# Two decoder layers with cross-attention: the attention's hand-written order runs to its end, the prologue's projections are reordered, feed-forward weights overlay the staging, four columns early

## The chip, the cores and the metric

One core of a Trainium2 chip runs the whole program in one launch. The metric is the device time of an execution in microseconds (us); the median of several runs is given. A hardware profile of one execution comes with it. Five engines run their own instruction queues in order: PE (TensorE, matrix products and transposes), DVE (VectorE), ACT (ScalarE), POOL (GpSimd) and SP (SyncE, which here issues all DMA transfers).

## The reference

The input `x` is 8 blocks of 128 tokens by 512 features. Four steps are added to it in turn, each on the layer norm of what is there:

```
x = x + L0_xattn(layernorm(x), ctx)      # one head, keys projected from ctx
x = x + L0_ffn(layernorm(x))             # linear layer plus one LoRA rank, chosen per token
x = x + L1_xattn(layernorm(x), ctx, mask)
x = x + L1_ffn(layernorm(x))
```

The change lies in the last two. `L1_xattn` has 32 query heads and 8 key/value groups of head size 128; within a block of 128 tokens

```
q = rmsnorm(x @ Wq.T) ; k = rmsnorm(ctx @ Wk.T) ; v = ctx @ Wv.T
p = softmax(q @ k.T / sqrt(128) + mask)
out = (p @ v) @ Wo.T
```

`L1_ffn` has integer weights: a matrix is `(w - z) * s`, with one `z` and `s` for each group of 128 input rows and each column. With 1792 hidden features,

```
out = (silu(x @ Wgate) * (x @ Wup)) @ Wdown
```

## The kernel before

Everything is float32 to the outside. A product is made from parts: an operand is cut into a rounded high part (`_h`, a copy on ScalarE) and the remainder (`_l`, a subtraction on VectorE), and `mm3` (lines 73 to 76) adds low x high, high x high and high x low in PSUM. So most cuts consist of a ScalarE instruction and a VectorE instruction that waits for it.

**Attention of the second layer.** The eight blocks are two halves (`hf`) of four. A unit `u` (64 of them, `NU`) is one kv group and one block: four query heads, 128 tokens. Four units share a key block (`k_load`, pool `pk`), a half-group of values (`v_load`) and a weight set of q and o (`wsets`). For one unit there are, in this order:

- `q_mm`: 12 matmuls of 128x512 into a bank of `ps_q` (tile `mm`, two banks); `q_ssq` squares on ScalarE; `q_rms` on POOL; `q_turn` scales and transposes on VectorE; `q_write` and `q_read` carry the result through DRAM, so that it comes back as `qT`.
- `s_mm`: scores, eight small matmuls; `s_max` (mask and maximum, VectorE); `s_exp` (four ScalarE instructions); `s_norm` (reciprocal on VectorE, product on POOL, tile `pr`).
- `p_mm`: four transposes on TensorE (tile `tr`); `p_cut`: `pT_h` on ScalarE, `pT_l` on VectorE; `av_mm`: three matmuls, the third of which reads `pT_l`; `av_cut`: `aT_h`, `aT_l`.
- `o_mm`: 12 matmuls; `o_add` adds to `xs`, the running `x`.

`round_(n)` (line 710) takes these steps for different units from the list `ROUND`, so that a round has one of each: `s_mm(n+1)`, `q_rms(n+3)`, `p_cut(n)`, `q_mm(n+4)` with its first k (three matmuls), `s_max(n+1)`, `av_mm(n)`, `av_cut(n)`, `q_turn(n+3)`, the rest of `q_mm(n+4)`, `s_exp(n+1)`, `o_mm(n)`, `s_norm(n+1)`, `q_ssq(n+4)`, `p_mm(n+1)`, `o_add(n)`. Between them run weight loads (`load`), weight cuts (`cut`: `wst` to the q or o set; pools `pst` and `pwq`/`pwo`), and the making of `w - z` for the feed-forward (`int`, `sub`), which goes to DRAM as `wint`.

**The order.** Inside `with tc.manual_schedule()` every engine's queue has the instructions in the order in which Python wrote them. Outside it a scheduler orders them by its own priorities. Before, the hand order covers a prologue (key/value groups 6 and 7, the first four `q_mm`, `s_mm(0)`) and rounds 0 to 50 (`LAST = 51`); rounds 51 to 63 and the two that follow are ordered by the scheduler. In the prologue each of three iterations has `q_mm(u)` first and then the two `kv_part` (a key/value projection of two blocks, 24 matmuls of 128x256) and `kv_out` (values and transposed keys to DRAM); `kv_w` loads and cuts a group's weights. Key/value groups 0 to 5 are made earlier, in scheduler order.

**The end of attention.** A block is finished when its last unit's `o_add` is done: units 52 to 55 finish the first half, 60 to 63 the second (`norms`). `layernorm_x` (bn_stats and aggr on VectorE, two POOL instructions for `rstd`, then `xn` on VectorE) follows at the end of that round; `layernorm_t` (four transposes into a bank of `ps_q`, `xnT_h` on ScalarE, `xnT_l` on VectorE) three rounds later for the first half, one for the second. With the first half normed, feed-forward columns (128 hidden features each, 14 of them) can begin: `early_unit` (line 634) makes one of four input groups of gate or up for one column, two matmuls of 128x512 into a bank of `ps_q` or `ps_s`; even groups are evacuated by ScalarE (L646), odd ones added on VectorE (L654) or, the last, by ScalarE and POOL (L651, L652); POOL adds the two sums, and tanh and two VectorE products make `early[c]`. `FILL` deals 24 such units (`NE = 3` columns) over the last rounds.

**The feed-forward.** `ORDER` lists the columns. An early column has only its second half of tokens to do. `weights` (L807) loads a column's `wint` into `wf_gate`, `wf_up`, `wf_down` (pool `fw`); `unit` (L816, L817) does its matmuls. Pools of SBUF are opened and closed as stacks from the left and the right, so what a new pool lies over must be free before its first write. Before, `fp` (gate and up sums) and `fw` are opened on the left after attention, in that order.

Of the kernel before, what the change touches and what calls it, by code (L numbers as in the profile page):

```python
# [9 lines left out]
F32 = mybir.dt.float32  # L10
# [7 lines left out]
P = 128  # L18
# [21 lines left out]
def tile_layers(ctx: ExitStack, tc: tile.TileContext, t, out: bass.AP):  # L40
    nc = tc.nc

    def pool(stack, name, bufs, space=None, side="left"):
        kw = {"side": side}
        if space is not None:
            kw["space"] = space
        return stack.enter_context(tc.tile_pool(name=name, bufs=bufs, reuse_waits="tile", **kw))
# [42 lines left out]
    def layernorm_t(xn, nh, nl, cols, ps_tr, extra=None, tag="tr"):  # L90
        tp = ps_tr.tile([P, KT, P], F32, name=tag)
        for k in range(KT):
            nc.tensor.transpose(tp[:, k, :], xn[:, k * P : (k + 1) * P], ident)
        nc.scalar.copy(nh[:, :, cols], tp)
        nc.vector.tensor_tensor(nl[:, :, cols], tp, f32(nh[:, :, cols]), ALU.subtract)
        if extra is not None:
            nc.scalar.copy(extra[:, :, cols], tp)
# [12 lines left out]
    xs = [const.tile([P, HB, D], F32, name=f"xs{hf}") for hf in range(2)]  # L110


    NE = 3
    LAG = 3
    skv = ctx.enter_context(ExitStack())
    cpool = pool(skv, "cpool", 1, side="right")
# [243 lines left out]

    kvw, kvo = {}, {}

    def kv_w(g):
        wst = kvp.tile([P, KT, 2 * HD], F32, name="wkv", bufs=1)
        nc.sync.dma_start(wst, t["kvT"][g].rearrange("(k p) n -> p k n", p=P))
        wh, wl = kvw[g] = tuple(kvp.tile([P, KT, 2 * HD], F32R, name=f"wkv_{p}") for p in "hl")
        for k in range(KT):
            split_fast(wh[:, k, :], wl[:, k, :], wst[:, k, :])
# [40 lines left out]
        nc.sync.dma_start(kT_d[g, hf], kb.rearrange("p j b a -> p j (b a)"))  # L409

    def kv_group(g):
        kv_w(g)
        for hf in range(2):
            for b0_ in (0, 2):
                kv_part(g, hf, b0_)
            kv_out(g, hf)
# [13 lines left out]
    l1s = ctx.enter_context(ExitStack())  # L430

    pst = pool(l1s, "pst", 5)
    pk = pool(l1s, "pk", 3)
    wk = pool(l1s, "wk", 2)
    pwq = pool(l1s, "pwq", 7)
    pv = pool(l1s, "pv", 2)
# [10 lines left out]
            wsets.append((g, HB * j))  # L447
        wset.append(len(wsets) - 1)
    NU = NG * NB
    FILL = {60: 3, 61: 4, 62: 7, 63: 4, 64: 12}  # L450
    xn1 = []
    wq, wo, kTt, vht, vlt = ({} for _ in range(5))
    qps, qss, rqs, qbs, q_d, qTs, sps, nms, sms, prs, tps, pTs, avs, aTs, pos = ({} for _ in range(15))
# [31 lines left out]
    def q_mm(u, ks):  # L485
        j, i = divmod(u, HB)
        v, cols = wset[j], slice(i * P, (i + 1) * P)
        nh, nl = xn1[blocks[j][1]]
        if ks[0] == 0:
            qps[u] = ps_q.tile([P, D], F32, name="mm")  # L490
        for k in ks:
            mm3(qps[u], nh[:, k, cols], nl[:, k, cols], *wq[v, k], k == 0, k == KT - 1)

    def q_ssq(u):
        ssq = qss[u] = small.tile([P, NREP], F32, name="qssq")
        for r in range(NREP):
            junk = wk.tile([P, HD], F32, name="junkq", bufs=2)
            nc.scalar.activation(  # L498
                junk, qps[u][:, r * HD : (r + 1) * HD], AF.Square, accum_out=ssq[:, r : r + 1]
            )  # L500

    def q_rms(u):
        rqs[u] = rms_factor(qss.pop(u), NREP, "q")
# [13 lines left out]
    def q_write(u):  # L517
        q_d[u] = dram.tile([P, NQ, NREP * SQ], F32, name=f"q_d{u}")
        nc.sync.dma_start(q_d[u], qbs.pop(u).rearrange("p j r a -> p j (r a)"))
# [37 lines left out]
    def p_mm(u):  # L557
        tp = tps[u] = ps_tr.tile([P, NQ, P], F32, name="tr")
        for r in range(NQ):
            nc.tensor.transpose(tp[:, r, :], prs[u][:, r, :], ident)  # L560
# [71 lines left out]
        nc.sync.dma_start(f32(et[m, c]), wint[m, c])  # L632

    def early_unit(m, g, c):
        if len(fill) < 10 and g % 2:
            ps = ps_s.tile([P, NREP, P], F32, name="s").rearrange("p r c -> p (r c)")
        else:
            ps = ps_q.tile([P, D], F32, name="mm")
        nh, nl = xn2[0]
        w = et[m, c][:, g * P : (g + 1) * P]  # L640
        nc.tensor.matmul(ps, w, nl[:, g, :], start=True, stop=False)
        nc.tensor.matmul(ps, w, nh[:, g, :], start=False, stop=True)
        s = (sg_sb if m == "gate" else su_sb)[:, c, g : g + 1]
        if g % 2 == 0:
            et[m, c, g] = wk.tile([P, NREP, P], F32, name="qT", bufs=8).rearrange("p r c -> p (r c)")
            nc.scalar.activation(et[m, c, g], ps, AF.Copy, scale=s)  # L646
        else:
            d = et[m, c, g - 1]
            if (m, g) in (("gate",3),("up",3)):
                a2 = wk.tile([P, NREP, P], F32, name="qT", bufs=8).rearrange("p r c -> p (r c)")  # L650
                nc.scalar.activation(a2, ps, AF.Copy, scale=s)  # L651
                nc.gpsimd.tensor_tensor(d, d, a2, ALU.add)  # L652
            else:
                nc.vector.scalar_tensor_tensor(d, ps, s, d, ALU.mult, ALU.add)  # L654
        if g == 3:
            nc.gpsimd.tensor_tensor(et[m, c, 0], et[m, c, 0], et[m, c, 2], ALU.add)
            if m == "gate":
                th = early[c] = fth.tile([P, TOK], F32, name="the")
                nc.scalar.activation(th, et[m, c, 0], AF.Tanh, scale=0.5)
                nc.vector.scalar_tensor_tensor(th, th, 1.0, et[m, c, 0], ALU.add, ALU.mult)  # L660
            else:
                th = early[c]
                nc.vector.scalar_tensor_tensor(th, th, 0.5, et[m, c, 0], ALU.mult, ALU.mult)

    tasks = {}

    def at(n, kind, fn, *a):
        tasks.setdefault((n, kind), []).append((fn, a))
# [13 lines left out]
        at(i, "int", int_dma, m, c)  # L682
        at(i + 1, "sub", int_sub, m, c)

    EW0 = min(FILL) - 2
    for c in range(NE):
        for m in ("gate", "up"):
            at(EW0 + c, "load", early_w, m, c)
    fill = [(m, g, c) for c in range(NE) for m in ("gate", "up") for g in range(KT)]

    def filler(n, k):
        m = FILL.get(n, 0)
        for _ in range(m * (k + 1) // 6 - m * k // 6):
            if fill:
                early_unit(*fill.pop(0))

    xn2, xnb = {}, {}
    norms = {}
    for b in range(NB):
# [8 lines left out]
    ]  # L708

    def round_(n):  # L710
        k = 0
        for it in ROUND:
            if isinstance(it, str):
                for fn, a in tasks.get((n, it), []):
                    fn(*a)
            elif 0 <= n + it[0] < NU:
                it[1](n + it[0], *it[2:])
            if not isinstance(it, str) and it[1] in (s_mm, s_max, av_mm, s_exp, o_mm, p_mm):
                filler(n, k)
                k += 1  # L720
        for b in [b for u, b in norms.items() if u == n - (3 if b < HB else 1)]:
            hf, i = divmod(b, HB)
            if i == 0:
                xn2[hf] = tuple(big.tile([P, KT, TOK], F32R, name=f"xnT_{p}") for p in "hl")
            layernorm_t(xnb[b], *xn2[hf], slice(i * P, (i + 1) * P), ps_q, tag="mm")
        b = norms.get(n)
        if b is not None:
            xnb[b] = layernorm_x(xs[b // HB][:, b % HB, :])

    nc.sync.dma_start(sg_sb, t["gsT"].rearrange("(c p) g -> p c g", p=P))  # L730
# [14 lines left out]
    k_load(*blocks[0])  # L745
    v_load(*blocks[0])


    LAST = 51
    with tc.manual_schedule():  # L750
        kv_w(NG - 2)
        for u, (g, hf) in enumerate(((NG - 2, 0), (NG - 2, 1), (NG - 1, 0))):
            q_mm(u, range(KT))
            q_ssq(u)
            kv_part(g, hf, 0)
            q_rms(u)
            if u:
                q_read(u - 1)
            kv_part(g, hf, 2)
            q_turn(u)  # L760
            q_write(u)
            kv_out(g, hf)
            if u == 0:
                kv_w(NG - 1)
            for k in ((0, 1), (2, 3), ())[u]:
                load_dma("o", 0, k)
        s_mm(0)
        s_max(0)
        s_exp(0)
        q_mm(3, range(KT))  # L770
        q_ssq(3)
        kv_part(NG - 1, 1, 0)
        s_norm(0)
        for fn, a in tasks[-1, "load"]:
            fn(*a)
        kv_part(NG - 1, 1, 2)
        kv_out(NG - 1, 1)
        skv.close()

        fth = pool(ctx, "fth", NE, side="right")  # L780
        pwo = pool(l1s, "pwo", 8, side="right")
        pat = pool(l1s, "pat", 2, side="right")
        ps_tr = pool(l1s, "ps_tr1", 2, PSUM)
        ps_o = pool(l1s, "ps_o", 2, PSUM)
        p_mm(0)
        for k in range(KT):
            load_cut("o", 0, k)
        for n in range(LAST):
            round_(n)
    for n in range(LAST, NU + 2):  # L790
        round_(n)
    l1s.close()

    fh = pool(ctx, "fh", LAG, side="right")
    fa = pool(ctx, "fa", 1, side="right")
    fp = pool(ctx, "fp", 2)
    fw = pool(ctx, "fw", 3)  # L800
    ps_f = pool(ctx, "ps_f", 4, PSUM)

    acc = fa.tile([P, KT, 2, TOK], F32, name="acc")
# [92 lines left out]
        nc.gpsimd.tensor_tensor(first_h[1][:, 0, :], early[c], f32(first_h[0][:, 0, :]), ALU.subtract)  # L896


    ORDER = [3,0,4,1,5]+list(range(6,14))+[2]
    for i in range(NI - NE):  # L900
        O_ = [NE + i] + list(range(NE))[i * NE // (NI - NE) : (i + 1) * NE // (NI - NE)]

    DOWN = {i: (i - LAG,) for i in range(LAG, NI + LAG)}

# [88 lines left out]
```

## Time and profile before

| | |
|---|---|
| runs before, us | 904.38 median of 3 (904.29 to 906.5) |
| the profiled execution, us | 909.4, span 907.6 |
| mean granted TensorE clock | 0.983 |
| TensorE busy | 859.1 us, 95% |
| TensorE weight loads | 722.1 us, 80% |
| VectorE busy | 622.7 us, 69% |
| ScalarE busy | 442.2 us, 49% |
| GpSimd busy | 519.5 us, 57% |
| DMA | 141.07 MB, mean 155 GB/s |

The page lists busy time by engine, then the span in 40 equal slices (a digit is the busy share in tenths; PEclk is the clock that the throttle granted to TensorE, in tenths of full speed), the DMA queues, the chain of work that ended last, and the costliest groups of instructions with what ended the idle time before them. In a timeline, a row has its start, its duration, the engine, the source line, what it writes and reads, and in brackets how long the engine had been idle and which engine's result ended that. In the windows view the columns after the window are its length and the busy time (and count) of PE, PEld, DVE, ACT and POOL, then the granted clock, the DMA engines' busy share and GB/s. Matmuls overlap in their pipeline, so a row's duration is longer than the distance to the next row.

Stages of the profiled execution: the first layer and key/value groups 0 to 5 to about 186 us; the hand-ordered prologue to about 231; the rounds to about 721; the first feed-forward matmul of the last stage starts at 739.08.

### The profile page before, as it was taken

The numbers are of one execution on the slowest core, as the hardware profiler recorded it, in microseconds if no ns is written. First come the engines' busy times: TensorE is split into PE (matmuls) and PEld (weight loads), VectorE is DVE, ScalarE is ACT, GpSimd is POOL, SyncE is SP. The second block draws the span as 40 slices with busy tenths as digits, with TensorE's granted clock in tenths as the row PEclk, the third lists the DMA queues.
The fourth block names the chain that finished last, engine by engine and source line by source line (L and its number), as shares of the span: only waits on it lengthen the run. The fifth ranks groups of instructions, "written<-read, shape, count | busy, mean of one in ns | idle before, by whom it ended". The sixth has DMA issues, their size and how long they took to land.

```text
span 907.6 us, 14436 instructions
## 1 busy us (share of the span) xinstructions
PE 859.1 (95%) x4568; PEld 722.1 (80%) x4568; DVE 622.7 (69%) x1047; ACT 442.2 (49%) x1573; POOL 519.5 (57%) x571
## 2 busy tenths in 40 slices
PE   6999999998899999999999999998999969999985
PEld 5889999888788888888888888886878647788854
DVE  6413897664677776677767766665686647988896
ACT  5324443134444444444444444444465449676652
POOL 4541784222375555555555555867643347899994
PEclk9899999999899999999999999999999979999998
DMA  8422441236787788788777876446421033222102
GB/s 295 127 94 95 151 151 60 82 118 204 231 243 227 228 244 237 222 237 245 232 232 230 236 223 214 138 153 186 150 90 60 0 116 92 65 76 70 47 23 94
DMA packets 141181, 141.07 MB, mean 155 GB/s; under 512 B 17968, under 2 KB 92464, under 8 KB 141104
## 3 DMA queue, kind: packets, MB, share of 16 engines
q1 hardware_dynamic: 141104, 140.14, 50.9%
q8 instruction: 37, 0.61, 0.3%
q14 instruction: 40, 0.33, 0.1%
HBM read 97.62 MB, written 42.47 MB: 154 GB/s over the span
## 4 chain that ended last, share of the span: by engine, by line
PE 68%; issue 9%; POOL 7%; DVE 7%; DMA 6%; ACT 1%; SPq 1%; DVEq 0%; POOLq 0%; ACTq 0%
PE f L816 8%; PE f L817 7%; PE mm L74 7%; PE mm L75 6%; PE mm L76 6%; PE o L76 5%; PE s L533 5%; PE o L74 5%; PE o L75 5%; DMA qT<-q_d 3%; PE tr L560 3%; PE o L574 1%; PE o L572 1%; PE o L573 1%; DMA q_d<-qb 1%
## 5 line engine op out<-in xcount | busy, mean ns | idle before, releaser
L555 POOL TENSOR_TENSOR pr<-pr,rs 128x512 f32<-128x512 f32 x64 | 66.6, 1041 | 163.9 <-DVE rs L553 163.1
L74 PE MATMUL mm<-wq_l,xnT_h 128*128 128x512 f32 x256 | 105.5, 412 | 1.0 <-DVE wq_l L66 1.0
L594 DVE TENSOR_TENSOR xs<-o,xs 128x512 f32<-128x512 f32 x64 | 44.2, 690 | 87.2 <-PE o L76 87.1
L74 PE MATMUL o<-wo_l,aT_h 128*128 128x512 f32 x256 | 100.8, 394 | 2.3 <-ACT aT_h L581 1.3
L76 PE MATMUL o<-wo_h,aT_l 128*128 128x512 f32 x256 | 100.5, 392 | 0.9 <-DVE aT_l L582 0.9
L76 PE MATMUL mm<-wq_h,xnT_l 128*128 128x512 f32 x256 | 100.5, 393 | 0.0
L75 PE MATMUL mm<-wq_h,xnT_h 128*128 128x512 f32 x256 | 100.4, 392 | 0.0
L75 PE MATMUL o<-wo_h,aT_h 128*128 128x512 f32 x256 | 99.8, 390 | 0.0
L547 ACT ACTIVATE pr<-s,nm 128x128 f32<-128x128 f32 x256 | 90.9, 375 | 13.1 <-DVE nm L541 10.7
L564 ACT CAST pT_h<-tr 128x512 fp32r<-128x512 f32 x64 | 37.5, 586 | 112.2 <-PE tr L560 112.2
L581 ACT CAST aT_h<-o 128x512 fp32r<-128x512 f32 x64 | 37.6, 587 | 105.4 <-PE o L574 105.4
L498 ACT ACTIVATE junkq<-mm 128x128 f32<-128x128 f32 x256 | 67.6, 279 | 22.9 <-PE mm L76 16.3
L74 PE MATMUL kv<-wkv_l,cT_h 128*128 128x256 f32 x256 | 73.6, 288 | 0.8 <-DVE kn L396 0.6
L76 PE MATMUL kv<-wkv_h,cT_l 128*128 128x256 f32 x256 | 73.3, 286 | 0.0
L75 PE MATMUL kv<-wkv_h,cT_h 128*128 128x256 f32 x256 | 72.8, 284 | 0.0
L533 PE MATMUL s<-kT,qT 128*128 128x128 f32 x512 | 69.2, 278 | 3.7 <-DMA qT<-q_d 3.7
L533 PEld LDWEIGHTS s<-kT,qT 128*128 128x128 f32 x512 | 63.9, 194 | 5.5 <-issue 3.4
L344 POOL TENSOR_TENSOR rrq<-msq,nhalf 128x4 f32<-128x4 f32 x64 | 65.0, 1016 | 5.0
L74 PEld LDWEIGHTS o<-wo_l,aT_h 128*128 128x128 f32 x256 | 48.1, 188 | 13.5 <-ACT aT_h L581 4.1
L565 DVE TENSOR_TENSOR pT_l<-tr,pT_h 128x512 fp32r<-128x512 f32 x64 | 44.1, 689 | 20.4 <-ACT pT_h L564 20.2
L76 PEld LDWEIGHTS o<-wo_h,aT_l 128*128 128x128 f32 x256 | 48.0, 188 | 12.0 <-DVE aT_l L582 2.2
L76 PEld LDWEIGHTS mm<-wq_h,xnT_l 128*128 128x128 f32 x256 | 48.2, 188 | 10.7
(220 smaller groups left out, 2459.7 us busy)
## 6 DMA issues: line engine op xcount, KB each, us to landing
q_d<-qb SPq DMA_DIRECT2D x64, 256.0 KB, 2.5
qT<-q_d SPq DMA_DIRECT2D x256, 64.0 KB, 3.2
wst<-in_qpT SPq DMA_DIRECT2D x36, 256.0 KB, 3.9
wst<-in_opT SPq DMA_DIRECT2D x36, 256.0 KB, 3.4
wkv<-in_kvT SPq DMA_DIRECT2D x8, 512.0 KB, 4.3
v_d<-vh SPq DMA_DIRECT2D x16, 256.0 KB, 2.1
v_d<-vl SPq DMA_DIRECT2D x16, 256.0 KB, 2.3
kT_d<-kT SPq DMA_DIRECT2D x16, 256.0 KB, 2.6
```

Source lines behind the costliest of these rows:

```text
L74: nc.tensor.matmul(o, ah, bl, start=start, stop=False)
L75: nc.tensor.matmul(o, ah, bh, start=False, stop=False)
L76: nc.tensor.matmul(o, al, bh, start=False, stop=stop)
L344: nc.gpsimd.tensor_tensor(r[:, :n], ms[:, :n], nhalf[:, :n], ALU.pow)
L498: nc.scalar.activation(junk, qps[u][:, r * HD : (r + 1) * HD], AF.Square, accum_out=ssq[:, r : r + 1])
L533: nc.tensor.matmul(sp[:, r, :], qTs[u][:, r, :], kTt[blocks[j]][:, :, i, :], start=True, stop=True)
L547: nc.scalar.activation(pr[:, r, :], sps[u][:, r, :], AF.Exp, bias=nms[u][:, r : r + 1], accum_out=sm[:, r : r + 1])
L555: nc.gpsimd.tensor_tensor(pr, pr, rs.unsqueeze(2).to_broadcast([P, NQ, P]), ALU.mult)
L565: nc.vector.tensor_tensor(pl, tps[u], f32(ph), ALU.subtract)
L594: nc.vector.tensor_tensor(x, pos[u], x, ALU.add)
L816: nc.tensor.matmul(ps[:, hf, :], w, rl, start=True, stop=False)
L817: nc.tensor.matmul(ps[:, hf, :], w, rh, start=False, stop=True)
```

## The change

- Prologue: `kv_w` becomes `kv_load` and `kv_cut`; group 6 is loaded and cut, and group 7 loaded, ahead of the hand order. Each iteration has its first `kv_part` at its head; `q_rms`, `q_turn`, `q_write` of a unit come one iteration later; `q_mm(3)` follows the last `kv_part`; the cuts of the first o set and `q_ssq(3)` come ahead of `p_mm(0)`.
- The hand order covers all 64 rounds, the remaining early units and the last norm. Early units come at two places of a round, after `s_mm` and after `av_mm`: 1 and 3 in rounds 60 to 62, 3 and 3 in round 63, 11 after it, the last norm's transposes, and 3 more. The norm's transposes come one round after `layernorm_x` for both halves.
- `NE` is 4: 32 early units. They take `ps_q` every third time and banks of `ps_s` and `ps_tr` otherwise, and `ps_q` alone from round 63 on. All odd groups are added on VectorE; POOL's sum follows one unit later, the tanh and the products four units later (`later`).
- `pk` has two buffers instead of three. `fw`, `fa`, `fh` are opened on the left in this order, `fp` on the right, so that `fw` lies over the staging tiles (`pst`, `pk`).
- `ORDER` becomes [4,0,5,1,6,2,7,...,13,3] from [3,0,4,1,5,...,13,2].

```diff
-    NE = 3
+    NE = 4
...
-    pk = pool(l1s, "pk", 3)
+    pk = pool(l1s, "pk", 2)
...
-    FILL = {60: 3, 61: 4, 62: 7, 63: 4, 64: 12}
...
     def early_unit(m, g, c):
-        if len(fill) < 10 and g % 2:
-            ps = ps_s.tile([P, NREP, P], F32, name="s").rearrange("p r c -> p (r c)")
+
+        i = len(fill)
+        if i >= LATE or i % 3 == 0:
+            ps = ps_q.tile([P, D], F32, name="mm")
         else:
-            ps = ps_q.tile([P, D], F32, name="mm")
+            p, n = ((ps_s, "s"), (ps_tr, "tr"))[i % 3 - 1]
+            ps = p.tile([P, NQ, P], F32, name=n).rearrange("p r c -> p (r c)")
...
-            if (m, g) in (("gate",3),("up",3)):
-                a2 = wk.tile([P, NREP, P], F32, name="qT", bufs=8).rearrange("p r c -> p (r c)")
-                nc.scalar.activation(a2, ps, AF.Copy, scale=s)
-                nc.gpsimd.tensor_tensor(d, d, a2, ALU.add)
-            else:
-                nc.vector.scalar_tensor_tensor(d, ps, s, d, ALU.mult, ALU.add)
-        if g == 3:
-            nc.gpsimd.tensor_tensor(et[m, c, 0], et[m, c, 0], et[m, c, 2], ALU.add)
...
+            nc.vector.scalar_tensor_tensor(d, ps, s, d, ALU.mult, ALU.add)
+
+    def early_sum(m, c):
+        nc.gpsimd.tensor_tensor(et[m, c, 0], et[m, c, 0], et[m, c, 2], ALU.add)
+
+    def early_gate(c):
+        th = early[c] = fth.tile([P, TOK], F32, name="the")
+        nc.scalar.activation(th, et["gate", c, 0], AF.Tanh, scale=0.5)
+        nc.vector.scalar_tensor_tensor(th, th, 1.0, et["gate", c, 0], ALU.add, ALU.mult)
+
+    def early_up(c):
+        th = early[c]
+        nc.vector.scalar_tensor_tensor(th, th, 0.5, et["up", c, 0], ALU.mult, ALU.mult)
...
+    def fillers(count):
+        for _ in range(count):
+            m, g, c = fill.pop(0)
+            early_unit(m, g, c)
+            for it in later:
+                it[0] -= 1
+            while later and later[0][0] <= 0:
+                later.pop(0)[1]()
+            if g == KT - 1:
+                later.append([1, lambda m=m, c=c: early_sum(m, c)])
+                later.append([4, lambda m=m, c=c: (early_gate if m == "gate" else early_up)(c)])
...
+    FILL = {}
+    for n in range(NU - 4, NU - 1):
+        FILL[n, s_mm], FILL[n, av_mm] = 1, 3
+    FILL[NU - 1, s_mm], FILL[NU - 1, av_mm] = 3, 3
+    LATE = len(fill) - sum(m for (n, f), m in FILL.items() if n < NU - 1)
...
-            if not isinstance(it, str) and it[1] in (s_mm, s_max, av_mm, s_exp, o_mm, p_mm):
-                filler(n, k)
-                k += 1
-        for b in [b for u, b in norms.items() if u == n - (3 if b < HB else 1)]:
...
+            if not isinstance(it, str):
+                fillers(FILL.get((n, it[1]), 0))
+        if n - 1 in norms:
+            norm_turn(norms[n - 1])
+        if n in norms:
+            b = norms[n]
             xnb[b] = layernorm_x(xs[b // HB][:, b % HB, :])
...
-    LAST = 51
+    kv_load(NG - 2)
+    kv_cut(NG - 2)
+    kv_load(NG - 1)
+
     with tc.manual_schedule():
-        kv_w(NG - 2)
         for u, (g, hf) in enumerate(((NG - 2, 0), (NG - 2, 1), (NG - 1, 0))):
+            kv_part(g, hf, 0)
+            if u:
+                q_rms(u - 1)
+                q_turn(u - 1)
+                q_write(u - 1)
+            kv_part(g, hf, 2)
             q_mm(u, range(KT))
+            kv_out(g, hf)
             q_ssq(u)
-            kv_part(g, hf, 0)
-            q_rms(u)
-            if u:
+            if u == 0:
+                kv_cut(NG - 1)
+            else:
                 q_read(u - 1)
-            kv_part(g, hf, 2)
-            q_turn(u)
-            q_write(u)
-            kv_out(g, hf)
-            if u == 0:
-                kv_w(NG - 1)
-            for k in ((0, 1), (2, 3), ())[u]:
-                load_dma("o", 0, k)
+                for k in ((0, 1), (2, 3))[u - 1]:
+                    load_dma("o", 0, k)
         s_mm(0)
+        kv_part(NG - 1, 1, 0)
         s_max(0)
         s_exp(0)
-        q_mm(3, range(KT))
-        q_ssq(3)
-        kv_part(NG - 1, 1, 0)
+        q_rms(2)
+        q_turn(2)
+        q_write(2)
         s_norm(0)
...
         kv_part(NG - 1, 1, 2)
+        q_mm(3, range(KT))
         kv_out(NG - 1, 1)
...
-        p_mm(0)
         for k in range(KT):
             load_cut("o", 0, k)
-        for n in range(LAST):
+        q_ssq(3)
+        p_mm(0)
+        for n in range(NU):
             round_(n)
-    for n in range(LAST, NU + 2):
-        round_(n)
+        fillers(len(fill) - 3)
+        norm_turn(NB - 1)
+        fillers(len(fill))
+        while later:
+            later.pop(0)[1]()
...
-    fh = pool(ctx, "fh", LAG, side="right")
-    fa = pool(ctx, "fa", 1, side="right")
-    fp = pool(ctx, "fp", 2)
     fw = pool(ctx, "fw", 3)
+    fa = pool(ctx, "fa", 1)
+    fh = pool(ctx, "fh", LAG)
+    fp = pool(ctx, "fp", 2, side="right")
...
-    ORDER = [3,0,4,1,5]+list(range(6,14))+[2]
+    ORDER = [c for i in range(NE - 1) for c in (NE + i, i)] + list(range(2 * NE - 1, NI)) + [NE - 1]
```

More of the change, by code (lines that the diff above doesn't have):

```diff
@@ L361, in tile_layers, with kv_load, kv_cut @@
     kvw, kvo = {}, {}
-    def kv_w(g):
-        wst = kvp.tile([P, KT, 2 * HD], F32, name="wkv", bufs=1)
+    def kv_load(g):
+        wst = kvw[g] = kvp.tile([P, KT, 2 * HD], F32, name="wkv", bufs=1)
         nc.sync.dma_start(wst, t["kvT"][g].rearrange("(k p) n -> p k n", p=P))
+    def kv_cut(g):
+        wst = kvw[g]
         wh, wl = kvw[g] = tuple(kvp.tile([P, KT, 2 * HD], F32R, name=f"wkv_{p}") for p in "hl")
@@ L411, in kv_group @@
     def kv_group(g):
-        kv_w(g)
+        kv_load(g)
+        kv_cut(g)
         for hf in range(2):
@@ L648, in early_unit @@
             d = et[m, c, g - 1]
-            if (m, g) in (("gate",3),("up",3)):
-                a2 = wk.tile([P, NREP, P], F32, name="qT", bufs=8).rearrange("p r c -> p (r c)")
-                nc.scalar.activation(a2, ps, AF.Copy, scale=s)
-                nc.gpsimd.tensor_tensor(d, d, a2, ALU.add)
-            else:
-                nc.vector.scalar_tensor_tensor(d, ps, s, d, ALU.mult, ALU.add)
-        if g == 3:
-            nc.gpsimd.tensor_tensor(et[m, c, 0], et[m, c, 0], et[m, c, 2], ALU.add)
[L657 to L663, printed above, removed]
+            nc.vector.scalar_tensor_tensor(d, ps, s, d, ALU.mult, ALU.add)
[8 more added lines that the diff above has]
+        nc.vector.scalar_tensor_tensor(th, th, 0.5, et["up", c, 0], ALU.mult, ALU.mult)
     tasks = {}
@@ L683, in tile_layers, with norm_turn @@
         at(i + 1, "sub", int_sub, m, c)
-    EW0 = min(FILL) - 2
     for c in range(NE):
         for m in ("gate", "up"):
-            at(EW0 + c, "load", early_w, m, c)
+            at(NU - 6 + c, "load", early_w, m, c)
     fill = [(m, g, c) for c in range(NE) for m in ("gate", "up") for g in range(KT)]
[L691 to L695, printed above, removed]
+    later = []
+    def fillers(count):
[9 more added lines that the diff above has]
+                later.append([4, lambda m=m, c=c: (early_gate if m == "gate" else early_up)(c)])
+    def norm_turn(b):
+        hf, i = divmod(b, HB)
+        if i == 0:
+            xn2[hf] = tuple(big.tile([P, KT, TOK], F32R, name=f"xnT_{p}") for p in "hl")
+        layernorm_t(xnb[b], *xn2[hf], slice(i * P, (i + 1) * P), ps_q, tag="mm")
+    FILL = {}
[3 more added lines that the diff above has]
+    LATE = len(fill) - sum(m for (n, f), m in FILL.items() if n < NU - 1)
     xn2, xnb = {}, {}
@@ L710, in round_ @@
     def round_(n):
-        k = 0
         for it in ROUND:
@@ L717, in round_ @@
                 it[1](n + it[0], *it[2:])
-            if not isinstance(it, str) and it[1] in (s_mm, s_max, av_mm, s_exp, o_mm, p_mm):
-                filler(n, k)
-                k += 1
-        for b in [b for u, b in norms.items() if u == n - (3 if b < HB else 1)]:
[L722 to L727, printed above, removed]
+            if not isinstance(it, str):
[4 more added lines that the diff above has]
+            b = norms[n]
             xnb[b] = layernorm_x(xs[b // HB][:, b % HB, :])
@@ L896, in first_half @@
         nc.gpsimd.tensor_tensor(first_h[1][:, 0, :], early[c], f32(first_h[0][:, 0, :]), ALU.subtract)
-    ORDER = [3,0,4,1,5]+list(range(6,14))+[2]
-    for i in range(NI - NE):
-        O_ = [NE + i] + list(range(NE))[i * NE // (NI - NE) : (i + 1) * NE // (NI - NE)]
+    ORDER = [c for i in range(NE - 1) for c in (NE + i, i)] + list(range(2 * NE - 1, NI)) + [NE - 1]
     DOWN = {i: (i - LAG,) for i in range(LAG, NI + LAG)}
```

## The prediction

> **What bounds the kernel now.** I read the page first (busy shares, then the slices), then TensorE's waits, then windows and timelines around the long waits.
>
> ```profile
> PE   6999999998899999999999999998999969999985
> PEclk9899999999899999999999999999999979999998
> ```
>
> One digit is 22.7 us. TensorE (95% of the span) is the bound nearly everywhere; a gain can only come from the slices with a 6 or 8, a loss from any stretch where TensorE starts to wait. TensorE's waits name the holes:
>
> ```profile
> PE f L816 <- DMA wf_gate<-wint_gate: 7.5, 1, 7.5
> PE tr L560 <- POOL pr L555: 4.6, 1, 4.6
> PE s L533 <- DMA qT<-q_d: 3.7, 4, 2.5
> ```
>
> Their places: 731.6 us (feed-forward start), 225.0 (first softmax of the prologue), 625.1 (where the hand order ends). Windows of 4 us show what the long hole costs beyond itself:
>
> ```profile
> 716.00:720.00 4.00, 3.02 (x13) 1.89 (x12) 3.66 (x8) 1.58 (x3) 0.73 (x2) 1.00 0.00 0
> 728.00:732.00 4.00, 2.70 (x13) 1.84 (x12) 2.81 (x5) 3.11 (x6) 3.81 (x3) 1.00 0.00 0
> 736.00:740.00 4.00, 0.92 (x2) 0.83 (x3) 0.18 (x1) 0.62 (x1) 1.26 (x1) 0.50 0.61 193
> 740.00:744.00 4.00, 4.00 (x11) 3.05 (x10) 0.00 (x0) 2.23 (x2) 0.00 (x0) 0.51 0.98 335
> 744.00:748.00 4.00, 4.00 (x19) 3.29 (x18) 2.57 (x2) 2.00 (x2) 0.39 (x1) 1.00 0.36 120
> ```
>
> Second number: TensorE busy; third from the end: granted clock. 740–744 is "busy" throughout, but at 0.51, with 11 matmuls where the next window has 19. Against these holes stand the steady rounds and the feed-forward, where TensorE has no gap:
>
> ```profile
> 588.60:611.20 22.60, 22.60 (x120) 19.14 (x119) 14.30 (x25) 11.16 (x54) 14.46 (x18) 1.00 0.49 152
> 800.00:820.00 20.00, 20.00 (x90) 16.55 (x89) 17.74 (x16) 14.57 (x14) 19.55 (x8) 1.00 0.21 67
> ```
>
> The first is three rounds, so 7.5 us each; the second gives 20/90 = 0.222 us per 128x512 matmul, with VectorE and GpSimd nearly full too.
>
> VectorE where a layer norm of the second half meets a round:
>
> ```profile
> 705.29 0.69 DVE L594 TENSOR_TENSOR xs<-o,xs 128x512 f32<-128x512 f32 x1 [0.99 <-PE o L76]
> 706.02 0.69 DVE L80 BATCH_NORM_STATS2 bnst<-xs 128x6 f32<-128x512 f32 x1
> 707.25 0.17 DVE L82 BATCH_NORM_AGGREGATE mv<-bnst 128x2 f32<-128x6 f32 x1
> 708.37 0.55 DVE L87 TENSOR_SCALAR xn<-xs,mv,rstd 128x512 f32<-128x512 f32 x1 [0.95 <-POOL rstd L85]
> 708.83 0.68 DVE L565 TENSOR_TENSOR pT_l<-tr,pT_h 128x512 fp32r<-128x512 f32 x1
> ```
>
> xn sits 0.95 us at the head of VectorE's queue waiting for GpSimd's rstd, and pT_l, which TensorE needs for its third av matmul, stands behind it. Near 640–670, for the first half's norms, the scheduler had put other ready work between aggr and xn; a written order cannot.
>
> **The change, part by part** (durations from the one profiled execution, 909.4 us with a span of 907.6; the runs' median 904.38 lies 5.0 lower, so I take the difference over to it).
>
> *1. Prologue.* The same TensorE instructions in another order: a key half-block ahead of each q_mm, q_rms/q_turn/q_write one iteration later, q_mm(3) last, the wo cuts ahead of p_mm(0). Before, 186–235 us loses 4.65 (tr on pr) + 0.98 (wq_l) + 0.61 (kn) + 0.18 (wkv_l) + 0.35 (pT_l) = 6.8, and half clock from 229.64 to 235.4: four transposes 0.91 for 0.44, eight s matmuls 1.56 for 0.81, seven 128x512 2.97 for 1.6, together 2.6. Sum 9.4. After: s_mm(0) no longer waits on a late s_max, and q_mm(3) (2.73) and two half-blocks (2.9 each) lie ahead of tr. I chain s_max 0.69+0.69, exp 1.50, q_rms(2) 1.28 and pr 1.04 on their engines: tr waits 1.3. Then pT_h stands behind four wo copies on ScalarE (0.58 each): 1.2; pT_l behind four wo subtractions (0.69 each): 1.7. Sum 4.2. SP: the load of key group 7 is issued before, wo's loads one iteration later, q_write(2) behind s_mm(0); each has a round or more before its reader. Gain 5.2 (3 if a kv bank waits for kn again, 6.5 if the wo cuts find their gaps).
>
> *2. Hand order to the end: norms of the first half.* Rounds 53–57. Zero is s_mm(55)'s start in round 54. TensorE: s 0.81, then q_mm(58)'s first three, whose bank the norm's transposes hold until xnT_l is written: ScalarE xnT_h at 0.21 (0.59), VectorE xnT_l at 0.85 (0.67), so q_mm starts at 1.57 instead of 0.81: 0.76 lost. VectorE goes on: bn 1.45, aggr 2.18, GpSimd's rstd 2.44–3.26 (0.19+0.55 and its start), xn 3.31, pT_l 3.77 to 4.46. TensorE had done q_mm (0.68) and two av (0.46) at 2.71 and waits until 4.51: 1.80 lost. So 2.56 in each of 54, 55, 56; 1.5 in 53 (no transposes yet), 0.76 in 57: 9.9. Queued behind xn besides pT_l: s_max, aT_l, all late with it, so nothing refills the gap.
>
> *3. Hand order to the end: rounds 60–63 and the drain.* There is no q_mm any more to cover anything (2.73 of TensorE work gone per round; four early units give 4 x 0.455 = 1.8). Round 60: the unit after s_mm has its ScalarE copy (0.69) ahead of pT_h in the queue, so av starts at 2.69 instead of 1.27: 1.42. pT_l 0.28. The next three units of this round share one PSUM bank, each waiting for the last one's evacuation (0.69–0.74 after a 0.39–0.5 matmul): 1.30 + 0.95. aT_l stands behind two evacuations of 0.74: o_mm waits 1.15. The next tr on pr: 0.25. Round sum 5.35. Likewise 61: 1.42+0.28+0.84+0.65+1.12 = 4.3; 62: 1.42+1.37+0.84+0.12+1.64 = 5.4; 63: 1.42+1.94+0.97+0.56 = 4.9 (pT_l here again behind xn's wait for rstd); the units after round 63: 1.37+0.36+1.21 = 2.9. Sum 22.9. The first feed-forward matmul then waits some 1.5 for the last evacuation.
>
> *Balance of this stretch.* Start of round 51 (618.77) to the first feed-forward matmul (739.08): 120.3 before. TensorE's work in it: nine rounds of 7.505, three of 4.66, one of 3.4, eight norm transposes of 0.44, 24 units of 0.455: 99.3. So 21.0 is lost before, the 7.5 hole and the 2.5 at 625 included, both gone after. After: 99.3 + 8 more units (3.6) = 102.9, plus 9.9 + 22.9 + 1.5 = 34.3: 137.2. Cost 16.9.
>
> *4. Overlay of the staging.* wf_gate/wf_up now lie where wst and the cut tiles were, last used by the wo cuts near round 57; nothing else is on the DMA queues then (share 0.00 from 716 to 736), so they land long before. Its hole is counted above; the half clock after it goes as well: twelve matmuls from 739.08 to 744.14 take 5.06 for 12 x 0.227 = 2.7. Gain 2.4. Two pk buffers for three cost nothing: a key block's buffer is last read by s_mm a round before its next load, and a load has five rounds. Cover gone, one load of 2–4 us would show once per block.
>
> *5. Fourth early column.* 16 matmuls leave the feed-forward: 16 x 0.222 = 3.6. ORDER has one more half column, whose GpSimd and VectorE work (7.5 and 7.6 for TensorE's 7.1) gives back 0.5. Gain 3.1 (0 if GpSimd's 19.6 of 20 decides everywhere).
>
> *Sum:* +16.9 − 5.2 − 2.4 − 3.1 = +6.2. Own time 909.4 + 6.2 = 915.6; on the median 910.6. Measured rows give each duration, but the queue order decides the sum: if the eleven units' bank waits overlap the queue waits they follow, 22.9 falls to about 17; if GpSimd's adds (1.27) delay rstd and pr further, it grows to 28. So its own range is 904–917.
>
> **The clock, weighed.** The trace: 4.65 and 7.53 us without a matmul are followed by 0.50; the 2.5 us at 625 and the 0.3–0.85 us pieces at 716–732 left 1.00. [...] I take 0, since 716–732 had such gaps at 1.00.
>
> **The rivals.**
> *A (0.63), as summed:* 910.6.
> *B (0.22), the written order holds:* what ends a wait on paper is overlapped on the chip (rstd comes in 0.3 us as in the scheduler's 640–670, the copies slot in before tr ends), so that the stretch loses about 16 instead of 34.3. Then −1.4 − 10.7 = −12: 892. Break-even is 28.1 lost. For it: 640–650 and 670–700 run gapless with the same instructions. Against: there the order is another one, and the 708.37 row shows the wait in just the order that is now written.
> *C (0.10), the gate swings:* +9 on A: 919.6.
> *D (0.05), the overlay frees nothing:* if the f loads still wait for the end of attention (a release in the same address range that comes late), 7.5 + 2.4 come back: 920.5.
>
> **How the numbers follow.** A's own range, 904–917, holds nine tenths of it; to reach 8 in 10 the range takes in C and D up to 920 and B's upper part: 897–920. About 0.3% (2.7 us) is what a measurement can tell from no change. Faster by more (under 901.7): B and a little of A, 0.23. Within: 0.11, A's lower edge and B's upper. Slower: the rest, 0.66.
>
> **What would show it.** Right: xn rows with 0.7–1.1 idle on rstd ahead of pT_l in rounds 53–56, rounds of about 10.4 us there and 11–12 in 60–63; av waits on pT_h of about 1.4; no f wait on a DMA; granted clock 1.00 at the feed-forward's start; no 4.6 wait near 225. Wrong: TensorE near 10 of 10 in 640–700, or fewer than 28 us lost between round 51 and the first f matmul (B); slices at 0.5–0.9 clock in rounds 60–63 (C); f waiting on wf_gate (D).

## The result and the profile after

The changed kernel takes 932.9 us (median of 4 runs, 928.4 to 934.1) against 905.4 for the kernel before (4 runs): ratio 1.0289, interval 1.0246 to 1.0333. It is slower, as forecast, but by 27.5 us where 6.2 was forecast, and 932.9 lies outside the range of 897 to 920. The profiled execution took 932.6 us, with a span of 930.7 and a mean granted clock of 0.976 (before: 0.983).

| stretch of the profiled executions, us | before | after | difference | forecast |
|---|---|---|---|---|
| start to round 51 (one round, 7.5 us, after `s_mm(51)`) | 618.8 | 616.8 | -2.0 | -5.2 |
| round 51 to first feed-forward matmul | 120.3 | 150.0 | +29.7 | +16.9 |
| first feed-forward matmul to the end | 168.5 | 163.9 | -4.6 | -5.5 |
| span | 907.6 | 930.7 | +23.1 | +6.2 |

The profiled execution of before was longer than its timed runs (909.4 against a median of 905.4), which is why the medians are 4 us further apart than the spans.

From the page of the changed kernel, busy share and granted clock in slices of 23.3 us:

```profile
PE   6999999996999999999999999998896779999985
PEclk9999999998999999999999999999999789999998
```

The prologue, two slices of 8 before, is now one of 6, and ahead of the feed-forward there is a row of 8, 8, 9, 6, 7, 7 in place of one 8 and one 6. TensorE's waits:

```profile
PE o L575 <- ACT pT_h L567: 11.6, 5, 6.6
PE o L577 <- DVE pT_l L568: 11.0, 7, 2.5
PE o L76 <- DVE aT_l L585: 2.9, 4, 1.0
PE mm L74 <- DVE xnT_l L95: 2.0, 4, 0.5
PE mm L93 <- DVE qT L655: 2.0, 1, 2.0
```

The wait for `wf_gate` is gone, and so is the one of tr on pr (now 1.1). In their place stand two groups for the halves of `pT`. One wait of 6.6 us is the prologue; the other four for `pT_h` are 1.25 us each, one in each of rounds 60 to 63. VectorE in round 54:

```profile
642.81 0.69 DVE L80 BATCH_NORM_STATS2 bnst<-xs 128x6 f32<-128x512 f32 x1
643.53 0.18 DVE L82 BATCH_NORM_AGGREGATE mv<-bnst 128x2 f32<-128x6 f32 x1
644.67 0.55 DVE L87 TENSOR_SCALAR xn<-xs,mv,rstd 128x512 f32<-128x512 f32 x1 [0.96 <-POOL rstd L85]
645.13 0.68 DVE L568 TENSOR_TENSOR pT_l<-tr,pT_h 128x512 fp32r<-128x512 f32 x1
```

This is the row pattern that the prediction described: 0.96 us of waiting for rstd with `pT_l` behind it. TensorE's third av matmul of that round starts at 645.86 after 1.50 idle, and the round takes 10.48 us (about 10.4 was forecast). What was not in the sum is the clock. Windows of 4 us in rounds 61 and 62 (second number TensorE busy, third from the end the granted clock):

```profile
712.00:716.00 4.00, 2.40 (x6) 1.63 (x7) 3.52 (x5) 0.77 (x2) 1.40 (x2) 0.82 0.79 231
724.00:728.00 4.00, 1.53 (x8) 0.67 (x6) 2.91 (x5) 1.23 (x3) 1.98 (x3) 1.00 0.41 131
728.00:732.00 4.00, 3.31 (x7) 2.00 (x7) 2.69 (x5) 0.77 (x2) 0.00 (x0) 0.52 0.26 66
732.00:736.00 4.00, 3.12 (x7) 1.71 (x7) 2.03 (x4) 1.80 (x9) 1.04 (x1) 0.50 0.00 0
736.00:740.00 4.00, 4.00 (x18) 3.30 (x17) 0.69 (x1) 0.21 (x1) 0.00 (x0) 0.70 0.00 0
```

After the window in which TensorE was busy for 1.5 of 4 us, some 10 us run at half clock: 7 matmuls in 4 us, 0.43 apart where they follow each other. Between 656 and 766 there are 45 such matmuls in five groups, within 23.9 us at half clock. Taking each one's distance to the next, less listed idle and less 0.2275, they cost 9.3 us together.

The prologue: ScalarE, SP and TensorE.

```profile
227.09 2.18 ACT L65 CAST wo_h<-wst 128x512 fp32r<-128x512 f32 x4 [5.81 <-issue]
230.18 0.59 ACT L567 CAST pT_h<-tr 128x512 fp32r<-128x512 f32 x1
```

```profile
223.84 0.75 SPq L405 DMA_DIRECT2D v_d<-vh  x1
224.69 0.38 SPq L406 DMA_DIRECT2D v_d<-vl  x1
```

```profile
221.95 0.66 PE L563 MATMUL tr<-ident,pr 128*128 128x128 f32 x4 [1.13 <-POOL pr L558]
230.83 0.79 PE L575 MATMUL o<-pT_h,vl 128*128 128x512 f32 x1 [6.63 <-ACT pT_h L567]
```

tr comes 7.7 us sooner than before, after the wait of 1.13 that was worked out as 1.3. But the wo copies, which stand ahead of `pT_h` on ScalarE, begin only at 227.09: the tile of the first `wo_h` lies on the SBUF of the last `vh`, and the write of that `vh` to DRAM was issued at 223.84, behind the key and value loads on SP. That write landed at 227.02. (That the copy waited for it is read from these times here; the profile names it in e2_pcut_first.) So a 4.65 us wait became one of 6.63, and the half clock with it lasts 10.2 us where it was 6.8.

### The profile page after: what moved, and what is told of

Read it like the earlier page. It is cut to its first block, busy times and chain, and to the rows that moved or that the text cites. A ratio compares the mean times of both kernels' runs of the same rounds, so it can differ in the third digit from the quotient of the medians.

```text
span 930.7 us, 14454 instructions
## 1 busy us (share of the span) xinstructions
PE 868.0 (93%) x4568; PEld 723.6 (78%) x4568; DVE 635.0 (68%) x1059; ACT 440.6 (47%) x1573; POOL 512.4 (55%) x568
```

## The experiments

Two theories after the result. W: the time is lost to waits that the written order makes, at the end and at the wo cuts. C, which belongs to it: part of the loss is the half clock that these waits bring on. The rivals: the fourth column, its PSUM banks or the overlay cost the time whoever orders it, or a repaired wait only changes its place. Times are medians; the kernel before, on the same chip, was at 905.3 for the first four, 906.8 for the next four and 906.2 for the last two. Differences to the changed kernel are to its 932.9; the kernel before moved by 1.5 between these series, so no more is read into small differences across them.

**e1_sched_end: the end given back to the scheduler.**

```diff
-        for n in range(NU):
+        for n in range(51):
             round_(n)
-        fillers(len(fill) - 3)
...
+    for n in range(51, NU):
+        round_(n)
+    fillers(len(fill) - 3)
```

> The changed kernel with only rounds 51 to 63, the last units and the last norm given back to the scheduler; prologue, overlay, fourth column and the places of the early units stay. Theory W (waits of the written order at the end, and the half clock they bring, make the loss): the stretch from round 51 to the first feed-forward matmul falls from 150.0 us to about 116-122, so some 30 less than the changed kernel: 900-906. Rival N (the fourth column, its banks and the overlay cost the time, whoever orders it): the stretch stays above 140, total above 922.

902.0 us, ratio to before 0.9945 (0.9921 to 0.9969): 30.9 less than the changed kernel, as W has it. Everything else of the change is still in it. The stretch from round 51 to the first feed-forward matmul takes 119.3 us. The weight loads of the feed-forward now go out at 697.10, and its first matmul comes at 735.06:

```profile
697.10 0.38 SPq L836 DMA_DIRECT2D wf_gate<-wint_gate  x1
```

```profile
735.06 0.76 PE L845 MATMUL f<-xnT_l,wf_gate 128*128 128x512 f32 x1 [2.69 <-issue]
```

The prologue's wait is the same as in the changed kernel (6.84). So the whole loss, and more, is the hand order from round 51 on. The scheduler's order has its own waits there (5.3 us for q through DRAM, and the 2.7 above, for which the profile names no cause) and two stretches at half clock, 13.7 us together, the second at the start of the feed-forward.

**e2_pcut_first: pT_h ahead of the wo cuts.**

```diff
+        p_mm(0)
+        p_cut(0)
         for k in range(KT):
             load_cut("o", 0, k)
         q_ssq(3)
-        p_mm(0)
```

(Round 0 then leaves its own `p_cut(0)` out.)

> The changed kernel with p_mm(0) and p_cut(0) written ahead of the four wo cuts. Theory W: the first av waited 6.6 us for pT_h only because pT_h stood behind wo_h copies, which waited for the key/value writes to DRAM (their SBUF lies under wo); now av starts by about 224.5, o_mm(0) waits up to 2 us for wo, no half clock follows: 6.5 to 9 less, 924-926. Rival: pT_h's own buffer lies over key/value staging too and waits for the same writes: 0 to 2 less.

927.5 us, 5.5 less; W, a little short of its range. av runs to 222.72 now, but then the first o_mm waits 3.56 us for `aT_h`, which stands behind the same wo copies, and 3.4 us at half clock follow, where none was expected. Here the profile names what the copies wait for:

```profile
225.09 2.18 ACT L65 CAST wo_h<-wst 128x512 fp32r<-128x512 f32 x4 [4.00 <-DMA v_d<-vh]
228.83 0.50 PE L74 MATMUL o<-wo_l,aT_h 128*128 128x512 f32 x1 [3.56 <-ACT aT_h L584]
```

The rival about `pT_h`'s own buffer is out.

**e3_xn_later: pT_l ahead of xn.**

```diff
         if n in norms:
             b = norms[n]
-            xnb[b] = layernorm_x(xs[b // HB][:, b % HB, :])
+            stats[b] = layernorm_s(xs[b // HB][:, b % HB, :])
...
+            if not isinstance(it, str) and it[1] is p_cut:
+                norm_x(n - 1)
```

(`layernorm_s` ends with `rstd`; `norm_x` writes `xn`, for the last block ahead of the last transposes.)

> The changed kernel with xn written after p_cut of the next round, so that VectorE takes pT_l before it waits for rstd. Theory W: the pT_l waits of 1.34, 1.50, 1.49, 1.50 in rounds 53-56 and of 0.77, 1.91, 2.52 in rounds 61-63 go (11 us), with most of the half clock that follows them (1.7 + 6): 12 to 18 less, 915-921. Rival Q (the wait only moves to s_max and aT_l, which then stand behind xn): 0 to 4 less.

922.2 us, 10.7 less. The waits for `pT_l` after 616 us fall from 11.0 to 0.3. The half-clock matmuls ahead of the feed-forward fall from 45 to 17 (9.3 to 3.5 us), but the last such stretch now runs on into the feed-forward and slows its first eight by some 1.7 us. And the edit put one new wait in: the last block's `xn` is written just ahead of the last transposes.

```profile
PE mm L97 <- DVE xn L91: 4.7, 1, 4.7
PE o L76 <- DVE aT_l L589: 4.1, 4, 1.8
PE o L581 <- DVE pT_l L572: 0.3, 1, 0.3
```

10.7 of waits and 4.1 of half clock, less 4.7, make 10.1. W for the mechanism, short of its size by the new wait and the half clock that stayed.

**e5_dummy_matmuls: more work in the gaps.**

```diff
+        first, pairs = {54: (0, 3), 55: (0, 3), 56: (0, 3), 60: (5, 0), 61: (5, 1), 62: (5, 4), 63: (5, 5)}.get(u, (0, 0))
+        for _ in range(first):
+            nc.tensor.matmul(av, vh, xn2[0][0][:, 0, :], start=True, stop=True)
+        for _ in range(2 * pairs):
+            nc.tensor.matmul(av, vl, ph, start=True, stop=True)
         nc.tensor.matmul(av, vl, ph, start=True, stop=False)
```

> The changed kernel with 64 extra 128x512 matmuls whose results are overwritten, put where TensorE stood idle: 5 before the first av of rounds 60-63, and 2 to 10 between that and the second in rounds 54-56 and 61-63. 14.5 us more of TensorE work at full clock. Theory C (the half clock of rounds 54-63 is set by idleness, about 10 us of loss): granted clock stays 1.00 there and the kernel gets 5 to 9 faster than the changed one although it does more: 924-928. Rival P (the clock falls for another reason, or a few idle pieces too short to matter): 0 to 4 slower.

926.9 us, 6.0 less with 58 matmuls more in the program (20 before the first av, 38 behind; the expectation's 64 was miscounted). Three windows at the same times as those shown above (the rounds lie within 2.5 us of those of the changed kernel):

```profile
724.00:728.00 4.00, 3.90 (x25) 3.17 (x24) 2.22 (x5) 1.75 (x3) 0.85 (x3) 1.00 0.29 86
728.00:732.00 4.00, 3.42 (x14) 2.18 (x12) 3.96 (x5) 0.44 (x1) 1.16 (x1) 1.00 0.22 68
732.00:736.00 4.00, 2.50 (x9) 1.50 (x10) 2.07 (x5) 2.13 (x10) 0.91 (x1) 1.00 0.14 43
```

Clock 1.00 where the changed kernel had 0.52 and 0.50. 18 half-clock matmuls remain, costing 3.7 us: those at 761–763, and a stretch at 705–711 that is new, for the changed kernel had 1.00 there (the last section takes it up). So 5.6 us of half clock went, about the gain of 6.0 by medians; the two profiled executions differ by 2.7. This supports C: work added to the gaps held the clock up at those places, and the rival, that nothing is gained by it, is out.

**e6_pcut_loads: the key and value writes ahead of the loads.**

```diff
-        for fn, a in tasks[-1, "load"]:
-            fn(*a)
         kv_part(NG - 1, 1, 2)
         q_mm(3, range(KT))
         kv_out(NG - 1, 1)
+        for fn, a in tasks[-1, "load"]:
+            fn(*a)
```

(on top of e2_pcut_first)

> e2_pcut_first with, in addition, the loads of the next key block written after kv_out of the last half-block instead of ahead of it. Theory W (wo_h and wo_l wait for the last key/value writes, and these stand on SP's queue behind 2.7 us of loads): aT_h's wait of 3.56 falls to about 1, the kernel is 2 to 3 faster than e2_pcut_first: 924-926. Rival (the writes are late because kn and its transpose are late, not because of SP): within 1 of e2_pcut_first, 926.5-928.5.

929.6 us, no better than e2_pcut_first (ratios to before 1.025 and 1.023, not told apart). The cause that was assumed is confirmed, the gain is not: the copies now start at 222.22, and the profile names the write, but the next score waits for its q, whose read stands behind the moved loads.

```profile
222.22 2.18 ACT L65 CAST wo_h<-wst 128x512 fp32r<-128x512 f32 x4 [0.19 <-DMA v_d<-vh]
```

```profile
233.26 1.13 PE L536 MATMUL s<-kT,qT 128*128 128x128 f32 x8 [2.10 <-DMA qT<-q_d]
```

The totals say little about this repair. Up to round 51 the two profiled executions are 0.5 us apart; most of their 3.9 arises behind it, where both have the same order, with 30.7 us at half clock here and 20.5 in e2_pcut_first.

**e7_sched_pcut_loads** is e1_sched_end and e6_pcut_loads together.

> e1_sched_end and e6_pcut_loads together: the scheduler orders the end, the prologue has p_mm(0) and p_cut(0) ahead of the wo cuts and the loads behind kv_out; overlay and fourth column stay. Theory W: the savings add: 902 - 8 = 893-896, some 10 under the kernel before. Rival R (a prologue that ends earlier only meets the same q_d and weight transfers later): 899-902.

898.6 us, ratio 0.9896 (0.9863 to 0.9929): between the two expectations. The wait for q is 4.1 us here.

**e8_overlay_only: on the kernel before, nothing but the order of the pools.**

```diff
-    fh = pool(ctx, "fh", LAG, side="right")
-    fa = pool(ctx, "fa", 1, side="right")
-    fp = pool(ctx, "fp", 2)
     fw = pool(ctx, "fw", 3)
+    fa = pool(ctx, "fa", 1)
+    fh = pool(ctx, "fh", LAG)
+    fp = pool(ctx, "fp", 2, side="right")
```

> The kernel before with only the feed-forward's pools reordered, so that fw lies over the staging. My prediction's step 4: the 7.5 us hole and 2.4 of half clock go, up to 2.7 remains as the wait for the last early unit as in e1_sched_end: 7 to 9 less, 896-898. Rival D (the loads still cannot start before the end, or the hole turns into a wait for the last early units): 902-906.

900.0 us, ratio 0.9929 (0.9907 to 0.9951): 6.9 under the kernel before. The hole of 7.53 is gone; the first feed-forward matmul comes at 730.59 instead of 739.08, after a wait of 1.70 for `xnT_l`, and without half clock behind it.

```profile
730.59 0.50 PE L816 MATMUL f<-xnT_l,wf_gate 128*128 128x512 f32 x1 [1.70 <-DVE xnT_l L95]
```

**e9_hand_repaired: the hand order with three repairs.** e3_xn_later and e6_pcut_loads, and:

```diff
-        FILL[n, s_mm], FILL[n, av_mm] = 1, 3
-    FILL[NU - 1, s_mm], FILL[NU - 1, av_mm] = 3, 3
+        FILL[n, p_cut], FILL[n, av_mm] = 1, 3
+    FILL[NU - 1, p_cut], FILL[NU - 1, av_mm] = 3, 3
```

> The changed kernel, hand order to the end, with the three repairs: xn behind p_cut, the first units of rounds 60-63 behind p_cut instead of ahead of it, and the prologue of e6_pcut_loads. Theory W: beyond e3_xn_later (922) the four pT_h waits of 1.25 go with some of their half clock (5 to 9 less) and the prologue's 8: 905-909, so still not under the kernel before, because bank and aT_l waits of rounds 60-63 and the drain remain. Rival Q (the waits only change place): 912-916.

918.0 us: 4.2 less than e3_xn_later (the intervals of the two ratios to before overlap), outside both expectations and nearer the rival's. After 615 us the waits for `pT_h`, 5.0 in e3_xn_later, are gone from the list; others have grown:

```profile
PE o L76 <- DVE aT_l L589: 6.2, 4, 2.3
PE mm L97 <- DVE xn L91: 4.7, 1, 4.7
PE mm L651 <- ACT qT L656: 2.3, 3, 0.8
```

With units behind `p_cut` the evacuations stand ahead of `aT_h` and `aT_l` instead of `pT_h`: the waits for `aT_l`, `aT_h` and `pT_l` have grown by 2.1, 0.6 and 1.5, so most of the 5.0 only moved. The 4.7 for `xn` is the wait that e3's edit made, and the half clock has not shrunk (20.5 us of it from round 51 on, 17.1 in e3_xn_later).

**e10_best4: e7 with the q read ahead of the loads.**

```diff
         kv_out(NG - 1, 1)
+        q_read(2)
         for fn, a in tasks[-1, "load"]:
```

(Round 0 then leaves its own `q_read(2)` out.)

> e7_sched_pcut_loads with q_read(2) written ahead of the loads that follow kv_out. Theory W: s(2)'s wait of 4.1 us for qT, and the half clock behind it (eight s matmuls in 2.05 us), came from that read standing behind loads on SP; they go, 4 to 6 less than e7_sched_pcut_loads: 892.5-895. Rival (q_d itself is written too late, the wait stays): 897.5-899.5.

896.9 us, ratio 0.9891 (0.9863 to 0.9919): not told apart from e7's 0.9896, where 4 to 6 us were expected. s(2) no longer waits, but s(3) does, at 239.69: the wait has gone on by a round, and shrunk from 4.1.

```profile
239.69 1.13 PE L536 MATMUL s<-kT,qT 128*128 128x128 f32 x8 [1.65 <-DMA qT<-q_d]
```

**e12_best3: the same with `NE = 3`.**

> e10_best4 with three early columns instead of four (24 units). My prediction's step 5 (the fourth column saves 3.1 in the feed-forward and costs 3.6 before it): within 1 of e10_best4. Rival E (the scheduler fits the eight extra units into gaps that TensorE has anyway at the end of attention): 2.5 to 4 slower than e10_best4. Rival F (the extra units lengthen the drain by bank waits): 2 or more faster.

895.8 us, ratio 0.9884 (0.985 to 0.9918), within 1.1 of e10_best4 and with overlapping intervals. The fourth column is worth nothing that can be measured here: in the profiled executions it makes the feed-forward 3.2 us shorter (3.1 was worked out) and the stretch from round 51 on 5.5 longer (3.6), though those two stretches had different amounts of half clock in them (10.2 us and 3.4). This is the lowest median of the study, with e10_best4 beside it: 10.4 under the kernel before and 37 under the changed one.

## Why the prediction was wrong

*Step 2, norms of the first half: right.* Worked out 2.56 a round; rounds 53 and 54 took 9.60 and 10.48 against 9.4 and 10.4 of the sum. Round 55 took 12.1, since eight of its matmuls ran at half clock.

*Step 3, rounds 60 to 63: the waits right, their consequence priced at nothing.* (The list of the change has one thing the wrong way round, which the sums have right: it is the units of rounds 60 to 62 that all take `ps_q`; from 739.51 on the trace shows them in banks of `ps_s`, `ps_q` and `ps_tr` in turn.) The list of waits after 616 us adds up to 28.1 us. The profile counts idle from a matmul's modelled end, 0.16 after the next could have followed (0.39 against 0.23), so the four `pT_h` waits worked out as 1.42 read 1.25. With 26 waits that is 4 us, and 28.1 becomes some 32, where 34.3 was forecast with pieces too small for the list. Work of 102.9 and waits of 34.3 give 137; the stretch took 150.0. Of the 13 missing, 9.3 are half clock. The rest, 3 to 6, is what longer matmuls and slower neighbours add to the waits: in rounds 61, 62 and 63 `pT_l` is waited for 0.77, 1.91 and 2.52 instead of 0.28, 1.37 and 1.94, for in each `xn` took 1.48 to 1.49 us beside a POOL addition (L658) that began 0.07 us before it (742.80 in round 63), where it takes 0.55 without one (644.67). That share is argued from rows, not tried.

*The step that failed first: the clock, "I take 0".* The runs show 9.3 us of half clock in its place. I followed one row: gaps at 716–732 of the kernel before had stayed at 1.00. More than half of the waits are for `pT_h` and `pT_l` (16.0 of 28.1). The price in rival C, +9 at one chance in ten, was an estimate whose terms no run shows; what the runs showed in its place are these 9.3 us. That the two are close is partly luck: 1.7 of the 9.3 lies in round 55, and the same order from round 51 on spent 23.9 us at half clock in this execution, 20.5 in e2_pcut_first and 30.7 in e6_pcut_loads. The row did not carry the argument: the windows of 716–732 had TensorE busy for 2.7 to 3.4 of 4 us, in rounds 61 to 63 of the changed kernel the windows of the same length ahead of the half clock have 1.5 to 2.4. My own sum of work and waits for these rounds puts them there, below nearly all that the kernel before had been seen to bear.

*Step 1, the prologue: failed.* Gain worked out 5.2, measured 2.0 at round 51 and 1.1 at `s_mm(2)`. Even that is not the prologue's: key/value groups 0 to 5 ended 1.0 earlier (184.32 for 185.28), so from there to `s_mm(2)` both kernels took 55.3 to 55.4 us. The term is "pT_h stands behind four wo copies: 1.2". The copies were costed by their durations alone; that their tile had to be free of the last key/value write, which SP issues behind the next loads, was not asked (in e2_pcut_first the first copy waits 4.00 us for that write). In the kernel before the wo copies started at 227.37 too, right behind the last `vh` copy, and cost nothing, since tr itself came only at 229.64.

*Step 4, the overlay: right in mechanism.* No wait on `wf_gate`, no half clock at the start. Measured alone on the kernel before it is 6.9 us; 7.5 + 2.4 less the new wait of 1.7 make 8.2. *Step 5: right that it is near nothing in sum* (worked out 3.6 more before, 3.1 less behind; e10 against e12: 1.1, not told apart).

*The rivals.* B, that the written order holds, is out by its own test (some 32 us of waits, not 16). C came true on top of A. D is out.

*Size.* Forecast +6.2; +3.2 up to round 51, +12.8 from the stretch, +0.9 from the feed-forward give the +23.1 between the two profiled executions. Nearly all of the other 4.4 of the 27.5 is that the profiled execution of before took 4.0 more than its median.

## What to carry to other kernels

Once an order is written out, each queue must be read for what stands behind an instruction that waits: a subtraction for the other engine's scalar (`xn` for `rstd`, 0.96 us at 644.67), a copy for a buffer that a DMA still reads (4.00 us in e2_pcut_first). Add up the idle pieces in windows of a few microseconds as well as in sum: where TensorE would be busy for only about half of such a window (here 1.5 to 2.4 of 4 us), half clock after it is a real possibility, and a row that stayed at full clock with more work in it (2.7 to 3.4 of 4 us) does not rule it out. And test the parts of a change apart, for here one part, the pools' order, was a gain of 0.7% that the hand order's 3% hid.

## What was not expected of the hardware

The clock fell without any long gap: the largest idle piece in the stretch was 2.52 us. In the changed kernel's trace the half clock of the stretch came in five pieces, from 656.51, 714.54, 728.19, 745.26 and 762.33 on; the third is 10.24 us long, the others 3.41. In the 3.41 us ahead of them TensorE was busy (by the profile's busy time) for 1.59, 1.39, 0.75, 0.73 and 1.25 us, in the last 3.41 us of each for 3.41, 3.35, 3.41, 3.01 and 3.41. Windows of that length in the changed kernel:

```profile
700.88:704.30 3.42, 2.05 (x7) 0.78 (x5) 2.25 (x4) 0.31 (x1) 0.00 (x0) 1.00 0.41 142
704.30:707.71 3.41, 1.96 (x7) 1.25 (x8) 2.12 (x4) 2.26 (x10) 0.00 (x0) 1.00 0.00 0
724.78:728.19 3.41, 0.75 (x3) 0.30 (x2) 2.42 (x5) 1.16 (x2) 1.98 (x3) 1.00 0.48 154
728.19:731.61 3.42, 2.92 (x6) 1.92 (x7) 2.50 (x4) 0.38 (x1) 0.00 (x0) 0.50 0.30 77
731.61:735.02 3.41, 2.53 (x5) 1.07 (x5) 2.03 (x4) 2.19 (x10) 0.35 (x1) 0.50 0.00 0
735.02:738.43 3.41, 3.41 (x9) 2.64 (x8) 0.00 (x0) 0.00 (x0) 0.69 (x1) 0.50 0.00 0
738.43:741.85 3.42, 2.72 (x16) 1.96 (x14) 2.09 (x4) 1.83 (x4) 0.00 (x0) 1.00 0.00 0
```

and in e5_dummy_matmuls:

```profile
701.78:705.19 3.41, 1.61 (x6) 0.61 (x5) 1.39 (x3) 1.16 (x3) 0.00 (x0) 1.00 0.15 56
705.19:708.60 3.41, 2.77 (x8) 1.72 (x7) 2.72 (x5) 1.41 (x9) 0.00 (x0) 0.50 0.00 0
```

In round 60 both kernels wait for a PSUM bank at the same times, for 1.02 us until 703.2 and for 0.78 until 704.8. In the changed kernel two windows that meet at 704.30, between the two waits, are busy for 2.05 and 1.96 of 3.4 us, and the clock stays at 1.00. In e5 both waits lie in the 3.41 us ahead of the half clock; TensorE is busy for 1.61 of them. A window as idle as that was not always followed by half clock: in the kernel before, in the 3.41 us from 621.01 on, with most of the 2.5 us on which the prediction leaned, TensorE is busy for 1.54, and the clock stayed at 1.00. What decides whether a given gap brings on half clock is not shown by these executions.

Matmuls whose results are thrown away kept the clock up (in e5_dummy_matmuls 1.00 at 728–736, where the changed kernel had 0.52 and 0.50), and the kernel got faster by doing more (926.9 us for 932.9). The changed kernel's own runs spread over 928.4 to 934.1, with mean clocks of 0.981 at the fastest and 0.972 at the slowest.
